# Queries and keys of an attention layer by fifteen products over thirds, in two passes of three heads, in place of seven products over halves in three passes of two

## The chip, the cores and the metric

One core of one Trainium2 chip. The metric is the device time of one run of the kernel, in microseconds, as the median of the runs shown. All numbers are float32.

## What is computed

Two graph layers over 128 graphs of 64 nodes with 768 features, 8192 rows in all. Each layer adds its attention's output to its input and normalizes.

```python
# layer 0: twelve heads of 64
h = jnp.einsum('bnd,ade->bane', feat_in, W); th = jnp.tanh(h)
attn = einsum(th, w_src) + swapaxes(einsum(th, w_dst), 2, 3)      # leaky, masked, softmax
feat_out = elu(einsum('banm,bame->bane', attn, h) + b)
gate = sigmoid(feat_in @ H_w.T + H_b)
x = layernorm(x + gate * feat_out + (1 - gate) * feat_in)
# layer 1: six heads of 128
q = heads(x @ Wq + bq); k = heads(x @ Wk + bk); v = heads(x @ Wv + bv)
probs = softmax(einsum('bhqd,bhkd->bhqk', q, k) / sqrt(128) + bias(mask), axis=-1)
x = layernorm(x + (einsum('bhqk,bhkd->bhqd', probs, v) merged) @ Wf + bf)
```

The change is in layer 1: how `x @ Wq` and `x @ Wk` are made, and what is ordered around them.

## The kernel before, in words

A tile is 128 rows (two graphs), a pair two tiles, a quad four tiles; there are 64 tiles, 32 pairs, 16 quads.

**Layer 0** runs over pairs: for each one the hidden product, the gate product and, two pairs behind, the product for layer 1's values, each over all 768 columns. Each is made by seven products of 384-wide halves instead of eight (the Strassen-Winograd form; `by_token`, L346, order in `TURNS`), each product three matmuls of 128x384. For the attention of each tile `attend` lists 33 steps on DVE, ACT, POOL, SP and PE. Transposes of rows and of weights go through DMA, on 2-byte halves of the numbers. When a pair is normalized, its transposed rows and their sums go to DRAM as the seven operands of the next layer (`ops_there`, L825 to L827), its values to `v_there`.

**Layer 1** runs over quads. Three times for each quad (`f` = 0, 1, 2), queries and then keys of two heads, `f` and `f + 3`, are made by seven products over halves (`by_feature`, L442: three matmuls of 128x256 each; `p1` to `p7` read the sums, two on ACT, five on DVE). After the last use of each of the seven blocks by `f` = 2, its `then` loads the block of the next quad into the same place in `zone` (L397). `slab` makes the scores of these two heads (L991), adds the mask (L1001), takes the softmax (L1005 to L1016), transposes the weights by DMA (L1031), makes the means (L1047) and transposes these by DMA (L1062) into the tiles `cT` (L1069). `output` makes the last product for two tiles at a time by fifteen products instead of eighteen: its contraction is cut in thirds, its columns in thirds, its rows in two (`FIFTEEN`; L1135, two matmuls of 128x256 a product, six sums in PSUM, of which two are taken up again by every third product). Every product is read and added to one or two of the six blocks of the result by DVE (L1148). Its operands on the side of the rows are sums that DVE makes (`operands`, L1102), those on the side of the weights sums that POOL makes once (L943). The rows that are added to come from DRAM (L1113), POOL adds the bias (L1118), and `normed` takes the statistics (DVE), the power (POOL, L370), the scaling (ACT, L1161) and the store.

**What sets the order.** Within an engine, instructions run in the order in which they were recorded. `Beat` sets it: a clock that runs on by one for every three matmuls; `beat.product` emits a product and sets its read 1.5 of its lengths later; lists of steps (`beat.start`, a `yield` is the pause) are emitted between the products at their times. It is an order alone, and the engines wait for each other through semaphores. All DMAs are issued by SP, one queue in that order. PSUM's eight banks: five for products, one for scores, two for means.

**At the border** of the layers the last pair's chain still runs while PE makes the values of the last pairs and, between these, queries and keys of quad 0; `matrix` loads and sums the weights of queries (POOL) and keys (DVE). **At the end** the two outputs of the last quad remain when the last scores are made; the operands of the first are DVE's, of the second mostly POOL's.

Of the kernel before, what the change touches and what calls it, by code (L numbers as in the profile page):

```python
# [54 lines left out]
P = 128  # L55
N = 64
# [18 lines left out]
PLACES = {X11: 0, X12: 1, X22: 2, S1: 3, S2: 4, S3: 5, S4: 6}  # L75

IN_ZONE = {X11: 0, S2: 1, S1: 2, X12: 3, S4: 4, X22: 5, S3: 6}


# [29 lines left out]


# [98 lines left out]
def two_layers(  # L209
# [68 lines left out]
    def matrix(w, name, engine, gap):  # L278

        t = places[place[name]]  # L280
        blocks = w.rearrange("(k c p) (m n) -> k m p c n", k=2, p=P, m=2)
        for at, k, m in ((W11, 0, 0), (T3, 0, 1), (W22, 1, 1), (W21, 1, 0)):
            for c in range(KH):
                nc.sync.dma_start(t[:, at, c], blocks[k, m][:, c])
                yield gap
        yield 3
        for to, a, b in ((T1, T3, W11), (T2, W22, T1), (T3, W22, T3), (N4, W21, T2)):
            for c in range(KH):
                engine.tensor_tensor(t[:, to, c], t[:, a, c], t[:, b, c], ALU.subtract)
                yield gap  # L290
        ready[f"{name}_sb"] = t


# [83 lines left out]
    ops_there = [dram.tile([P, 2, 7 * KH, P], F32, name=f"ops_there_{q}") for q in range(n_quads)]  # L377
# [3 lines left out]
    zone = const.tile([P, 7 * KH * 2 * P + 8 * P * 2], F32, name="zone")  # L381
# [10 lines left out]
    def load_block(q, k):  # L392

        at = PLACES[k] * KH
        t = in_zone(IN_ZONE[k] * D, KH, 2, P)
        for i in range(2):
            nc.sync.dma_start(t[:, :, i, :], ops_there[q][:, i, at : at + KH, :])  # L397
        return t.rearrange("p c i t -> p c (i t)")

    def queries(q, f, blocks, part):  # L400
        quads[q]["qT"] = in_zone(7 * KH * 2 * P, 2, 4 * P)
        by_feature(f"q_{q}_{f}_", blocks, ready["wq_sb"], f, bq_sb, quads[q]["qT"], part)

    def keys(q, f, blocks, part, then=None):
        quads[q]["kT"] = in_zone((7 * KH + 4) * 2 * P, 2, 4 * P)
        by_feature(f"k_{q}_{f}_", blocks, ready["wk_sb"], f, bk_sb, quads[q]["kT"], part, then)

    def by_feature(name, blocks, w, f, b_sb, r, part, then=None):

        sums = [sb(dense[0], [P, BANK], "dense", f"{name}{i}") for i in range(3)]  # L410
        begun = set()
        lo, hi = b_sb[:, f : f + 1], b_sb[:, f + 3 : f + 4]
        T = 2 * P
        u = {}

        def more(i, ps):
            u[i] = part(f"{name}u{i}")[:, 0:T]
            nc.vector.tensor_tensor(u[i], u[1], ps, ALU.add)

        def p1(ps):  # L420
            u[1] = part(f"{name}u1")[:, 0:T]
            nc.scalar.copy(u[1], ps)  # L422

        def p2(ps):
            nc.scalar.activation(r[:, 0, 0:T], ps, AF.Identity, bias=lo)

        def p7(ps):
            nc.vector.scalar_tensor_tensor(r[:, 1, T : 2 * T], ps, hi, u[3], ALU.add, ALU.add)

        def p4(ps):  # L430
            nc.vector.scalar_tensor_tensor(r[:, 0, T : 2 * T], ps, lo, u[1], ALU.add, ALU.add)

        def p3(ps):
            nc.vector.scalar_tensor_tensor(r[:, 1, 0:T], ps, hi, u[2], ALU.add, ALU.add)

        reads = dict(P1=p1, P2=p2, P3=p3, P4=p4, P5=lambda ps: more(3, ps), P6=lambda ps: more(2, ps), P7=p7)
        for what, to, xb, wb in TURNS:
            ps = sums[to][:, 0:T]

            def emit():  # L440
                for c in range(KH):
                    nc.tensor.matmul(  # L442
                        ps,
                        lhsT=w[:, wb, c, f * P : (f + 1) * P],
                        rhs=blocks[xb][:, c, :],
                        start=(c == 0 and to not in begun),
                        stop=(c == KH - 1),
                        skip_group_check=True,
                    )

            read = reads[what]
            beat.product(emit, lambda read=read, ps=ps: read(ps))
            begun.add(to)
            if then:
                then(xb)

    def phase_a(pa, ps_a, dst_pool):
# [25 lines left out]
        w_dst_sb = row(w_dst, "w_dst_sb", pa)  # L485
# [4 lines left out]
        w_src_sb = row(w_src, "w_src_sb", pa)  # L490
        h_b_sb = row(h_b, "h_b_sb", pa)
# [9 lines left out]
        for to, vector in ((bv_sb, bv), (bq_sb, bq), (bk_sb, bk)):  # L501
# [4 lines left out]
            [pa.tile([P, D], F32, name=f"{n}_{i}") for i in range(2)]  # L506
            for n in ("th_d", "bc_e", "xg_parts", "elu_turned", "gate", "mix")
        )
        h_of_tile = [pa.tile([P, H0, EP], F32, name=f"h_{i}") for i in range(3)]
# [300 lines left out]
        def sums_of_pair(p, begin):  # L810
# [12 lines left out]
            def away():  # L823
                there = ops_there[p // 2][:, p % 2]
                nc.sync.dma_start(there[:, 0 : 2 * KH], xo[:, 0:2].rearrange("p k c t -> p (k c) t"))  # L825
                nc.sync.dma_start(there[:, 2 * KH : 3 * KH], xo[:, 3])
                nc.sync.dma_start(there[:, 3 * KH : 7 * KH], so.rearrange("p k c t -> p (k c) t"))  # L827
# [79 lines left out]
    def phase_b(pb, ps_b):  # L907
# [75 lines left out]
        def slab(Q, f):  # L983
# [87 lines left out]
            if f == 2:  # L1071
                Q["done"] = True
# [181 lines left out]
```

## Time and profile before

| | us |
|---|---|
| three runs | 2860.69, 2854.07, 2859.43 |
| median | 2859.43 |
| the profiled execution: span from first to last instruction | 2857.3 |
| a pair of layer 0, steady | 42.75 |
| a quad of layer 1, steady | 87.8 |

The page gives no time for the profiled execution beside its span; it lies 2.1 us under the median and inside what the runs differ by. How to read it: PE is a matmul, PEld the load of its weights, which runs beside it. A float32 matmul has two records. L346 is any product of layer 0, L442 one of queries or keys, L1135 one of the output. A group's mean is the duration of one instruction from its start; on PE, where they overlap, its busy time divided by its records is nearer to what one costs. "Idle before" with a name behind it is the time in which the engine stood and what ended that. The waits are lines of who, for whom: total, times, longest.

### The profile page before, as it was taken

What the parts mean: (1) busy time and instruction counts of PE and PEld (TensorE: products, weight loads), DVE (VectorE), ACT (ScalarE), POOL (GpSimd) and SP (SyncE); (2) the same over time, 40 slices, a digit from 0 to 9 for tenths busy, and PEclk for the clock granted to TensorE, in tenths of its full rate; (3) what the DMA queues carried; (4) which work ended last, traced back from release to release, by engine and by line L of the source; (5) the groups of instructions that cost most, each with busy time, mean ns of one, the idle gap of its engine ahead of it and who ended that gap; (6) DMA issues with size and microseconds to landing.
All of it is one profiled execution on the core that took longest, in us unless ns stands there. A gap on an engine that the chain in (4) does not pass through costs nothing.

```text
span 2857.3 us, 43775 instructions
## 1 busy us (share of the span) xinstructions
PE 2803.1 (98%) x16168; PEld 2039.0 (71%) x16168; DVE 2042.6 (71%) x4103; ACT 1309.1 (46%) x1562; POOL 1063.8 (37%) x938
## 2 busy tenths in 40 slices
PE   7899999999999999999899999999999999999998
PEld 4555555555555555555588888888888888888886
DVE  6888888888888888888635556565555655556556
ACT  2655655655655655655423333333333333333331
POOL 5656656656656656666422101011011110110102
PEclk9999999999999999999999999999999999999999
DMA  6666666666666666667764345544355353554531
GB/s 202 160 167 175 171 173 171 177 163 173 179 162 175 178 167 170 178 167 191 206 156 117 97 110 128 128 95 107 100 132 135 92 122 85 123 135 99 124 87 58
DMA packets 627014, 409.59 MB, mean 143 GB/s; under 512 B 440177, under 2 KB 573041, under 8 KB 626801
## 3 DMA queue, kind: packets, MB, share of 16 engines
q1 hardware_dynamic: 626800, 406.81, 55.2%
q8 instruction: 127, 2.08, 0.3%
q14 instruction: 87, 0.70, 0.1%
HBM read 186.69 MB, written 119.93 MB: 107 GB/s over the span
## 4 chain that ended last, share of the span: by engine, by line
PE 90%; DMA 2%; DVE 2%; ACT 1%; issue 1%; SPq 1%; POOL 0%; POOLq 0%; DVEq 0%; ACTq 0%
PE o L1135 15%; PE q L442 14%; PE v L346 14%; PE h L346 14%; PE k L442 14%; PE g L346 14%; PE f_all L742 2%; PE s_ps L991 2%; PE c_ps L1047 2%; DMA s<-parts 1%; DMA th_d<-bc_e 0%; DMA elu_turned<-xg_parts 0%; DMA sT<-parts 0%; PE bias_ps L951 0%; DMA ops_there<-x_even 0%
## 5 line engine op out<-in xcount | busy, mean ns | idle before, releaser
L370 POOL TENSOR_TENSOR rs<-rs,power 128x1 f32<-128x1 f32 x128 | 73.8, 576 | 1097.3 <-DVE rs L368 1097.3
L346 PE MATMUL h<-w,zone 128*128 128x384 f32 x1320 | 447.9, 495 | 21.6 <-ACT h L533 12.5
L442 PE MATMUL q<-zone,w 128*128 128x256 f32 x2016 | 460.1, 383 | 4.7 <-issue 1.2
L346 PE MATMUL g<-w,zone 128*128 128x384 f32 x1320 | 441.0, 489 | 3.6 <-DVE gate L587 3.6
L442 PE MATMUL k<-zone,w 128*128 128x256 f32 x2016 | 443.2, 379 | 0.9 <-ACT k_u L422 0.9
L442 PEld LDWEIGHTS q<-zone,w 128*128 128x128 f32 x2016 | 379.8, 191 | 64.1 <-issue 8.7
L442 PEld LDWEIGHTS k<-zone,w 128*128 128x128 f32 x2016 | 383.2, 190 | 53.1 <-ACT k_u L422 1.3
L346 PEld LDWEIGHTS h<-w,zone 128*128 128x128 f32 x1320 | 251.3, 193 | 194.5 <-ACT h L533 13.8
L346 PEld LDWEIGHTS g<-w,zone 128*128 128x128 f32 x1320 | 247.9, 190 | 175.4 <-DVE gate L587 13.1
L1135 PE MATMUL o<-w,sc 128*128 128x256 f32 x1364 | 317.3, 381 | 5.0 <-DVE sc L1102 5.0
L1148 DVE TENSOR_TENSOR y<-y,o 128x256 f32<-128x256 f32 x512 | 207.2, 415 | 124.6 <-PE o L1135 119.8
L1135 PEld LDWEIGHTS o<-w,sc 128*128 128x128 f32 x1364 | 259.9, 191 | 41.6 <-DVE sc L1102 6.0
L346 PE MATMUL v<-w,x_sums 128*128 128x384 f32 x768 | 258.5, 487 | 1.7 <-DVE x_sums L315 1.6
L1118 POOL TENSOR_TENSOR y<-y,bf_sb 128x768 f32<-128x768 f32 x64 | 117.2, 1841 | 314.3 <-DMA y<-x_there 290.8
L662 POOL TENSOR_TENSOR bc_e<-th_d,w_dst_sb 128x768 f32<-128x768 f32 x64 | 120.7, 1886 | 292.3 <-ACT th_d L557 269.4
L346 PEld LDWEIGHTS v<-w,x_sums 128*128 128x128 f32 x768 | 145.8, 190 | 103.9 <-DVE x_sums L315 2.9
L1009 ACT ACTIVATE s<-s 128x512 f32<-128x512 f32 x48 | 30.2, 630 | 242.1 <-DVE s L1007 242.1
L1102 DVE SCALAR_TENSOR_TENSOR sc<-cT 128x256 f32<-128x256 f32 x217 | 116.6, 537 | 32.4 <-ACT cT L1069 32.4
L1061 ACT COPY parts<-c_ps 128x1024 uint16<-128x1024 uint16 x94 | 90.6, 1015 | 106.2 <-PE c_ps L1047 106.2
L657 POOL TENSOR_SCALAR zone<-zone 128x768 f32<-128x768 f32 x64 | 137.1, 2142 | 0.0
L1135 PE MATMUL o<-w,cT 128*128 128x256 f32 x512 | 132.6, 392 | 0.0
L650 ACT ACTIVATE gate<-gate 128x768 f32<-128x768 f32 x64 | 53.9, 843 | 167.6 <-DVE gate L593 118.6
(162 smaller groups left out, 4596.3 us busy)
## 6 DMA issues: line engine op xcount, KB each, us to landing
zone<-ops_there SPq DMA_DIRECT2D x224, 192.0 KB, 4.1
zone<-in_xT SPq DMA_DIRECT2D x32, 768.0 KB, 6.3
zone<-in_x SPq DMA_DIRECT2D x64, 384.0 KB, 3.8
bc_e<-there SPq DMA_DIRECT2D x128, 192.0 KB, 3.4
x_there<-mix SPq DMA_DIRECT2D x64, 384.0 KB, 3.9
ops_there<-x_sums SPq DMA_DIRECT2D x32, 768.0 KB, 3.3
v_there<-v SPq DMA_DIRECT2D x128, 192.0 KB, 2.6
v<-v_there SPq DMA_DIRECT2D x128, 192.0 KB, 3.8
```

Source lines behind the costliest of these rows:

```text
L346: nc.tensor.matmul(ps, lhsT=blocks[xb][:, c, :], rhs=w[:, wb, c, :], start=(c == 0 and to not in begun), stop=(c == KH - 1), skip_group_ch ...
L370: nc.gpsimd.tensor_tensor(rs[:, 0:1], rs[:, 0:1], power, ALU.pow)
L442: nc.tensor.matmul(ps, lhsT=w[:, wb, c, f * P : (f + 1) * P], rhs=blocks[xb][:, c, :], start=(c == 0 and to not in begun), stop=(c == KH - 1),
L657: nc.gpsimd.tensor_scalar(xs, xs, 1.0, None, ALU.add)
L662: nc.gpsimd.tensor_tensor(bc, th, w_dst_sb, ALU.mult)
L742: nc.tensor.matmul(f_all[b * N : (b + 1) * N, at : at + E0 + 1], lhsT=e[rows, hd // 2 * P + b * N : hd // 2 * P + (b + 1) * N], rhs=(h[row ...
L991: nc.tensor.matmul(s_ps[b * N : (b + 1) * N, i, r, :], lhsT=qT[:, r, at], rhs=kT[:, r, at], start=True, stop=True,)
L1061: nc.scalar.copy(by_halves(parts), halves(c_ps[:, r].rearrange("p i t -> p (i t)")))
L1102: nc.vector.scalar_tensor_tensor(s[:, k], of[a], sign, of[b], ALU.mult, op)
L1118: nc.gpsimd.tensor_tensor(y, y, bf_sb, ALU.add)
L1135: nc.tensor.matmul(ps, lhsT=of[xb][:, c, :], rhs=wf_sb[:, wb, c, :], start=(c == 0 and not begun), stop=(c == 1), skip_group_check=True,)
L1148: nc.vector.tensor_tensor(part_of, part_of, ps, ALU.add if sign > 0 else ALU.subtract)
```

## The change

Queries and keys are now made as the output is: fifteen products over thirds of the contraction, here with thirds for the three heads of a pass and two for the pairs of a quad. So there are two passes (`r` = 0, 1) of three heads. The first of a product's additions to a block is ACT's, with the bias, the others are DVE's. What goes to DRAM after layer 0 is the plain transposed rows; the eleven sums of them are POOL's, made for the whole quad from the loaded thirds in `zone` while the output of the quad before runs. For quad 0's first pass the eighteen plain products are made, from weights that are not yet summed. Two products have the sign of their weights turned, so that all of `X_SUMS` are plain sums. The scores of a pass stand after the second product of the next one, in two halves of three heads; the load of the next quad's mask stands beside them. The last tile rows, bias, pools' waits and the order at the border and at the end are changed with it.

```diff
+X_SUMS = (
+    ("3", "A0", "A2", ALU.subtract),
+    ("12", "3", "A3", ALU.add),
+    ("2", "A5", "A4", ALU.subtract),
...
+FREED = {"A2": "A2", "A5": "A5", "A3": "A3", "5": "A0", "A1": "A1", "6": "A4"}
...
+    def sums_of_quad(q):
+        there, made = quads[q].setdefault("raw", set()), set()
+        for name, a, b, op in X_SUMS:
+            while name in ("5", "6") and "raw_used" not in ready or not all(n in there or n in made for n in (a, b)):
+                yield 0.5
+            to, a, b = (operand(n).rearrange("p a b c -> p (a b c)") for n in (name, a, b))
+            nc.gpsimd.tensor_tensor(to, a, b, op)
+            made.add(name)
+            yield 0.5
...
+    def by_feature(name, w, r, b_sb, to_all, then=None):
+        sums, seen = {}, set()
+        for at, xb, wb, to in FIFTEEN:
...
+            def emit():
+                for c in range(2):
+                    nc.tensor.matmul(
+                        ps,
+                        lhsT=w[:, wb, c, r * P : (r + 1) * P],
+                        rhs=operand(xb)[:, c].rearrange("p i t -> p (i t)"),
+                        start=(c == 0 and not begun),
+                        stop=(c == 1),
+                        skip_group_check=True,
+                    )
...
+            def read(ps=ps, to=to):
+                for sign, b in to:
+                    m, n = divmod(b, 3)
+                    part_of = to_all[:, n, m * 2 * P : (m + 1) * 2 * P]
+                    if b in seen:
+                        nc.vector.tensor_tensor(part_of, part_of, ps, ALU.add if sign > 0 else ALU.subtract)
+                    else:
+                        seen.add(b)
+                        bias = b_sb[:, 3 * r + n : 3 * r + n + 1]
+                        nc.scalar.activation(part_of, ps, AF.Identity, bias=bias, scale=float(sign))
+            beat.product(emit, read, 2 / 3)
+            if then and xb in FREED:
+                then(FREED[xb])
...
             def away():
-                nc.sync.dma_start(there[:, 0 : 2 * KH], xo[:, 0:2].rearrange("p k c t -> p (k c) t"))
-                nc.sync.dma_start(there[:, 2 * KH : 3 * KH], xo[:, 3])
-                nc.sync.dma_start(there[:, 3 * KH : 7 * KH], so.rearrange("p k c t -> p (k c) t"))
+                nc.sync.dma_start(there, xo.rearrange("p k c t -> p (k c) t"))
...
-                beat.start(matrix(wq, "wq", nc.gpsimd, 0.6), 7)
-                beat.start(matrix(wk, "wk", nc.vector, 0.6), 14)
+                ready["wq_used"] = ready["wk_used"] = False
+                beat.start(first_blocks(), 4)
+                beat.start(by_head(wq, "wq", nc.gpsimd, 0.3), 7)
+                beat.start(by_head(wk, "wk", nc.vector, 0.5), 18)
+                beat.start(sums_of_quad(0), 21)
...
+        plain("q_0_0_", ready["wq_raw"], 0, bq_sb, qk[:, 0])
+        ready["wq_used"] = True
         value(n_pairs - 2)
-        queries(0, 0, blocks, part)
-        keys(0, 0, blocks, part)
+        beat.until(lambda: "wk_raw" in ready)
+        plain("k_0_0_", ready["wk_raw"], 0, bk_sb, qk[:, 1])
+        ready["wk_used"] = ready["raw_used"] = True
...
+        def slab(Q, r):
+            q, last = Q["q"], Q["q"] + 1 == n_quads and r == 1
+            if r == 1 and q + 1 < n_quads:
+                load(quads[q + 1])
...
+        for q in range(n_quads):
+            final = q + 1 == n_quads
+            if q:
+                queries(q, 0)
+                keys(q, 0)
...
+            beat.start(slab(Q, 0), 0.25)
+            if before:
+                beat.start(rows_of(before, 0))
+                beat.start(operands(before, 0))
+            queries(q, 1)
+            if not final:
+                if before:
+                    give(0)
+                beat.start(sums_of_quad(q + 1), 4)
+            if before:
+                beat.start(rows_of(before, 1))
+                beat.start(operands(before, 1), 6 if final else 0)
...
+            keys(q, 1, None if final else (lambda name: load_third(q + 1, name)))
+            beat.start(slab(Q, 1), 0.25)
+            if final:
+                beat.start(rows_of(Q, 0))
+                give(0)
+                beat.start(rows_of(Q, 1))
+                beat.start(operands(Q, 0), 1)
+                beat.start(operands(Q, 1), 6)
+            if before:
+                give(1)
             before, Q = Q, quads.get(q + 1)
+        give(0)
+        give(1)
...
-        tc.tile_pool(name="pb", bufs=1) as pb,
+        tc.tile_pool(name="pb", bufs=1, reuse_waits="tile") as pb,
```

`plain` is the same product without sums: for each half of the rows and each head six matmuls into one bank, read once by ACT. `give(i)` emits `output` for one half of the quad before, from its operands. So the passes of a steady quad are, in order: queries 0, keys 0, queries 1, first output, keys 1, second output. Each of the passes over queries or keys has fifteen products of two matmuls; the means of a pass stand in the passes after it, in two halves of three heads. Five banks of PSUM hold products, three scores, transposes and means.

## The prediction

> **What bounds the kernel now.** I read the page's busy table and its chain first, then the groups by form, then busy time by stretches, then the waits and the instructions of one quad in order of time.
>
> ```profile
> PE 2803.1 (98%) x16168; PEld 2039.0 (71%) x16168; DVE 2042.6 (71%) x4103; ACT 1309.1 (46%) x1562; POOL 1063.8 (37%) x938
> PE 90%; DMA 2%; DVE 2%; ACT 1%; issue 1%; SPq 1%; POOL 0%; POOLq 0%; DVEq 0%; ACTq 0%
> ```
>
> The chain that ended last is PE for 90%. The stretches (length, then busy PE, PEld, DVE, ACT, POOL with counts, clock, DMA share, GB/s) say where it isn't:
>
> ```profile
> 1351.41:1437.63 86.22, 74.81 (x343) 48.30 (x337) 57.07 (x102) 35.09 (x35) 35.01 (x32) 0.96 0.69 190
> 1621.64:1709.47 87.83, 87.83 (x566) 75.85 (x565) 51.48 (x123) 31.15 (x46) 10.59 (x12) 1.00 0.45 114
> 2796.82:2849.47 52.65, 47.13 (x249) 39.13 (x247) 36.37 (x89) 5.81 (x7) 13.46 (x19) 0.94 0.13 45
> 2849.47:2857.30 7.83, 0.00 (x1) 0.00 (x0) 2.44 (x10) 2.05 (x2) 1.49 (x4) 0.77 0.25 100
> ```
>
> The second row is one steady quad of layer 1: PE has no hole, DVE is busy for 59%, POOL for 12%. The first is the border of the layers, the third the end, the fourth the tail after the last matmul. So in layer 1 a matmul less is its time less, as long as no read of a product comes late.
>
> **What the skill says.** "SBUF — State Buffer", Who interferes with whom: a VectorE instruction with two SBUF inputs and a GpSimd instruction that reads SBUF exclude each other, whoever comes second waits for the whole instruction. The trace agrees: L1102 usually takes 0.42 us, and under a POOL addition
>
> ```profile
> 1640.51 1.81 POOL L1118 TENSOR_TENSOR y<-y,bf_sb 128x768 f32<-128x768 f32 x1 [5.15 <-DMA y<-x_there]
> 1640.78 1.82 DVE L1102 SCALAR_TENSOR_TENSOR sc<-cT 128x256 f32<-128x256 f32 x1
> ```
>
> "DMA: Bandwidth & Descriptors", Queues, rings and completion order: an issuing engine has one ring per DMA engine, consumed in order; so a small transfer stands behind large ones issued before it. The mask load had no such neighbours and still cost DVE 44.7/14 = 3.2 us a time (below). "TensorE: Matmul & The Clock Gate", Part 1: after some 3.4 us of idling the clock falls to half. The stretch 1400 to 1425, after a hole of 6.85 us, shows a granted clock of 0.87.
>
> **Part by part.** The rows I price with:
>
> ```profile
> L442 PE MATMUL k<-zone,w 128*128 128x256 f32 x2016 | 443.2, 379 | 0.9 <-ACT k_u L422 0.9
> L1148 DVE TENSOR_TENSOR y<-y,o 128x256 f32<-128x256 f32 x512 | 207.2, 415 | 124.6 <-PE o L1135 119.8
> L425 ACT ACTIVATE zone<-q,bq_sb 128x256 f32<-128x256 f32 x48 | 22.5, 468 | 66.5 <-PE q L442 66.1
> L943 POOL TENSOR_TENSOR w<-w 128x512 f32<-128x512 f32 x15 | 19.7, 1329 | 33.1 <-DMA w<-in_wf 32.7
> DVE biasb L972 <- DMA a8b<-in_adj: 44.7, 14, 5.1
> ```
>
> *Matmuls.* A matmul is two records; in the chain 42 records of k take 9.06 us, so 0.4314 us a matmul of 256 columns. A quad had 2 x 3 x 21 = 126 for queries and keys, and gets 2 x 2 x 30 = 120: 2.59 us less. Quad 0 gets 72 (plain) + 60 = 132. In all 2016 become 1932: 84 x 0.4314 = **-36.2 us**. Scores and means stay 96 matmuls a quad; groups of them stay six, so a quad without stalls is 87.8 - 2.6 = 85.2 us.
>
> *Reads.* A quad had 30 on DVE and 12 on ACT, and gets 40 of 0.415 and 24 of 0.469. DVE: 16.6 - 13.7 = +2.9 us of 85, ACT +6.3. Hidden as busy time. But a sum is now taken up again after two products (2 x 0.863 = 1.73 us), so a read that ends later holds PE. The output passes have lived on that distance already and PE waited for their reads only 0.5 us in all; there all reads are DVE's.
>
> *Sums by POOL.* 11 a quad of 1.33 us (L943) = 14.6 us in a row, during the second output pass, itself 14.6 us long (15 products of 0.863 and the scores, 1.08 x 1.5). They wait for the third loaded last; I count POOL ready about 17 us after the keys end, and the next queries need its late sums at 14.6 + 8.6 = 23 us. Not on the path in a steady quad. Its price is the exclusion above: two slab instructions of 128x768 (0.95 us, two SBUF inputs) can each be held up to 1.33 us, with reads queued behind.
>
> *The slab.* Two of 768 wide for three of 512: DVE 2 x 4.9 against 3 x 3.4 us, nothing. Its scores come after two products (1.73 us) where three of 1.29 covered the last keys before; one DVE read of 0.42 fits. The wait for the mask moves into the second output pass, ahead of that pass's first reads. I follow the pass: the load is issued about 0.9 us into it, behind 12 loads of 128 KB; it lands at 2.7 us if as quick as its 2.2 us so far, at 4.6 if it has to follow those (4.1 us; both medians from the page's DMA issues). The first read is needed at 4.2. Cost 0 to 1.1, and 0.3 for the exclusion: 0.3 to 1.4, I take 0.8.
>
> *ACT in the second keys pass.* Between the reads of products 8 and 10 stand one scaling (0.93) and two copies of 768 (L1069's pairs of 512 take 1.38, so 0.96 for one of 768). From 6.95 us: 0.38 + 0.93 + 1.92 + 0.47 + latency = 10.7, needed at 10.36: 0.36 us. In the first queries pass the transposed weights (issued at its start, 3.8 us to landing like the page's 12-block transpose th_d) come just ahead of need, 0 to 0.5, taken as 0.1. First keys, second queries and first output pass: 0. Sum **1.3 us a quad** (0.3 to 3), x 15 = **+19.5 us**.
>
> *SP, loads.* The 14 block loads become 12, spread over the second keys pass as slots come free; the writes of layer 0 shrink from seven blocks to four. Layer 0's order on PE is unchanged up to the last pair: 0.
>
> *Border.* Its 86.22 us held 9.87 + 3 x 13.54 + 2 x 9.06 + 2 x 1.06 = 70.7 us of products: 15.5 lost, most of it a weight transpose queued in SP behind ten zone loads (hole 6.85 us, and half clock after it). The loads are now early and the two plain passes are 15.5 us each, so these holes go. New ones: POOL makes 13 sums for wq (17.3 us) ahead of the power of the last tile, which I find ready at 71 us after the pair's begin and done at 82; scaling, transpose and copies end at 91.4, the last value product needs their sum at 89.5: 3.1 us. And in quad 1 no output pass covers POOL: its sums, with three of wf's between, end about 40.6 us after the second keys of quad 0 began, and the queries would be through at 37.8: 4.6 us. With 1.5 us of low clock 9.2: **-6.3**, from -12 to 0.
>
> *End.* 52.65 us held 90 output products' matmuls, a score group (1.28) and the last transposes and means (0.60 + 2.05): 90 x 0.4314 + 3.9 = 42.7: 9.9 lost to DVE making operands while PE waits. Now two output passes of the quad before (26 us) cover slab and operands (some 24.5 beats of 1.29 us, the first needed at beat 20), and POOL makes the second half. 2 us stay: **-7.9**. The tail of 7.83 us has the same steps.
>
> Sum: -36.2 + 19.5 - 6.3 - 7.9 = **-30.9**. The profiled execution spans 2857.3; the median of the runs, 2859.4, is 2.1 above that, which I leave: 2857.3 - 30.9 + 2.1 = **2828.5 us**.
>
> **Rivals.**
> 1. *All covered.* The mask lands in time and the reads hold, as they do in the output passes of before: no 19.5, so 2809. For: PE's waits for DVE there, 0.5 us. Against: ACT's 0.36 and POOL's lock follow from durations.
> 2. *Half eaten.* 2.7 us a quad (mask late, both locks met): +21, 2849.5.
> 3. *Slower.* The reads of the second output pass: DVE there has 16 x 0.335 + 5 us of slab + 3.2 of statistics = 13.6 us of 14.6, all behind the mask's wait, with POOL reading throughout. If the mask comes at 5 us or more and a lock is met at both 768 instructions, it can't catch up and PE follows it. It decides at (36.2 + 6.3 + 7.9) / 15 = 3.4 us a quad; at 4.5: 2859.4 + 67.5 - 50.4 = 2876.5. Against: in 1621 to 1709 two such locks of 1.4 us passed with PE at 100%.
> 4. *It doesn't do what it says*: out, since the order of the built kernel shows 966 matmuls each for q and k where there were 1008.
>
> **Chances.** Forecast (2818 to 2842) 0.42; rival 1 0.25; rival 2 (2842 to 2863) 0.18; rival 3 0.15. The range leaves out some of rivals 1 and 3: 2803 to 2865. A difference under 0.3% (8.6 us) can hardly be told from none here. Faster by more: 0.42 + 0.25 + half of rival 2 = 0.76; within: 0.10; slower: 0.14.
>
> **What would show it.** Right: a steady quad of 86.5 us (85.2 if rival 1, 88 or more if 2 or 3) with PE waiting for DVE reads of the second output pass and for ACT reads of keys; POOL at 30% in layer 1; the waits of the two-input slab instructions 1 us longer than bare; a hole of some 3 us before the last values and some 4 in quad 1's first queries; products until 8 us before the end. Wrong: a PE wait for transposed weights or for operands loaded late, a hole at the border of 10 us, or PE without holes in the steady quads at other than 0.43 us a matmul.

## The result and the profile after

The changed kernel takes 2844.27 us (median of 4 runs, 2841.36 to 2845.68) where the kernel before took 2858.61 (4 runs): a ratio of 0.9951, 95% interval 0.9937 to 0.9965. That is 14.3 us less; 30.9 were forecast. The profiled execution, the shortest of its four, spans 2839.6 us where before's spanned 2857.3: 17.7 less. The comparisons below are made between profiled executions and by stretch, since a median moves by 3 us from one set of runs to the next.

The page's busy table and chain, after:

```profile
PE 2777.5 (98%) x16002; PEld 2001.9 (71%) x16002; DVE 2111.3 (74%) x4182; ACT 1379.1 (49%) x1725; POOL 1316.8 (46%) x1119
PE 87%; DVE 5%; issue 2%; POOL 1%; DMA 1%; ACT 0%; SPq 0%; DVEq 0%; POOLq 0%; ACTq 0%
```

PE has lost 166 records and 25.6 us of busy time, and DVE stands in the chain with 5% where it had 2%: part of what PE no longer does is waited for instead. The same by stretches of the changed kernel: the border up to the last value product, one steady quad, the last 90 matmuls of the output (three passes of 15 products), the tail (length, then busy time of PE, PEld, DVE, ACT, POOL, the granted clock, DMA share, GB/s):

```profile
1351.41:1446.28 94.87, 85.35 (x396) 59.16 (x395) 61.29 (x92) 38.48 (x44) 59.96 (x46) 0.96 0.55 147
1696.49:1783.49 87.00, 86.14 (x553) 73.24 (x552) 54.66 (x129) 35.47 (x56) 26.65 (x24) 1.00 0.41 102
2783.73:2831.49 47.76, 46.02 (x232) 39.08 (x230) 33.58 (x93) 6.91 (x8) 16.72 (x25) 1.00 0.18 67
2831.49:2839.58 8.09, 0.00 (x0) 0.00 (x0) 2.44 (x10) 2.05 (x2) 1.48 (x4) 0.71 0.25 97
```

The steady quad takes 86.94 us on average (from one group of scores to the same group a quad later, over 13 quads), where 86.5 was forecast. By the same measure the kernel before takes 88.16, not the 87.8 of the single quad that the prediction started from, so the quad is 1.22 us shorter where 1.3 was forecast. In six of the runs below that leave the steady quads alone this figure is 87.0 to 87.2, so differences of 0.2 us a quad come from one execution to the next. POOL is busy for 30% in the quad. The border is not: PE lacks 9.5 of its 94.87 us. The rows that the prediction took its prices from held, but for POOL's sums, which took 1.43 instead of 1.33 us:

```profile
L520 PE MATMUL k<-zone,w 128*128 128x256 f32 x1860 | 414.3, 382 | 2.8 <-DVE qk L534 2.8
L538 ACT ACTIVATE qk<-k,bk_sb 128x256 f32<-128x256 f32 x186 | 88.3, 475 | 106.7 <-PE k L520 106.6
L474 POOL TENSOR_TENSOR zone<-zone 128x512 f32<-128x512 f32 x176 | 246.9, 1428 | 142.5 <-DMA zone<-ops_there 131.7
```

The wait of DVE for the mask (us in all, times, longest) was 44.7 us in 14 before, and is halved, though it now lies in an output pass:

```profile
DVE biasb L1052 <- DMA a8b<-in_adj: 21.2, 14, 4.9
```

**Where the 17.7 us come from.** Each term is the change of the time of that stretch, without what its larger or smaller number of matmuls accounts for:

| Term | Predicted | Measured | How measured |
|---|---|---|---|
| 84 fewer matmuls | -36.2 | -36.3 | records of each form x their undisturbed distance from start to start |
| layer 0 up to its last hidden product | 0 | -0.8 | its end, 1346.75 and 1345.99; over the other runs it lies at 1345.9 to 1348.2 |
| border, up to the last value product | -10.9 | -2.8 | 90.14 and 100.29 us, with 42 and 72 matmuls of quad 0 |
| steady stalls, and quad 1 | +19.5 + 4.6 | +24.9 | not measured by itself: the rest of the 17.7 |
| end, last 90 matmuls of the output | -7.9 | -3.0 | 52.65 us with scores and transposes in it, and 47.43 with 2.2 of these just ahead of it |
| tail | 0 | +0.3 | 7.8 and 8.1 us |

So 8 us are missing at the border and 5 at the end; the quads, where most of the argued risk lay, came out near the forecast.

**The border.** The largest hole in PE's timeline of the changed kernel, with the idle time ahead of the row and its releaser in brackets:

```profile
1401.64 0.34 PE L835 MATMUL f_all<-h,bc_e 64*64 64x65 f32 x1 [6.29 <-POOL w L341]
```

The hole before f_all, 6.85 us before, is there again with 6.29. The row names POOL's sums as its end; ACT's and SP's timelines, of which these are four rows, tell another story:

```profile
1385.93 1.47 ACT L819 COPY bc_e<-th_d 128x1536 uint16<-128x1536 uint16 x1
1391.70 3.83 SPq L328 DMA_DIRECT2D w<-in_wk  x6
1395.64 1.54 SPq L823 DMA_TRANSPOSE th_d<-bc_e  x1
1399.62 1.92 ACT L826 COPY bc_e<-th_d 128x1536 uint16<-128x1536 uint16 x1 [10.66 <-DMA th_d<-bc_e]
```

The block that is to be turned is ready at 1387.4. SP issues the loads of the key weights (each 0.6 us and more) and reaches the transpose at 1395.64; ACT's copy of what it brings ends at 1401.54, 0.1 us before f_all. The zone loads have left this place in SP's queue; the key weights' loads, begun at beat 18, have taken it.

**A steady quad.** PE's stalls in one quad of the changed kernel:

```profile
1704.54 5.45 PE L520 MATMUL q<-zone,w 128*128 128x256 f32 x24 [0.19 <-DVE qk L534]
1732.05 6.31 PE L520 MATMUL k<-zone,w 128*128 128x256 f32 x28 [0.18 <-DVE qk L534]
1748.37 1.99 PE L1230 MATMUL o<-w,sc 128*128 128x256 f32 x8 [0.48 <-DVE y L1243]
```

The brackets understate it. From start to start two records of PE (a matmul has two) are 0.216 us apart; at the first of these rows 0.57, and the next after it 0.32, so the stop costs 0.46. I sum this excess by pass; some 0.1 of each figure is the switch between kinds of matmuls, which the kernel before had too:

| us a quad | second queries | second keys | second output | scores to scores, us |
|---|---|---|---|---|
| changed kernel | 0.58 | 0.56 | 0.88 | 86.94 |
| y rows a pass earlier | 0.57 | 0.40 | 0.92 | 86.83 |
| maximum first | 0.14 | 0.29 | 0.90 | 86.38 |
| mask early | 0.57 | 0.56 | 0.70 | 86.79 |
| POOL's sums in halves | 0.57 | 0.57 | 0.30 | 86.37 |
| no sums by POOL | 0.57 | 0.57 | 0.11 | 86.17 |
| joined (below) | 0.10 | 0.28 | 0.23 | 85.68 |

The other three passes of a quad in the changed kernel, first queries, first keys and first output, have 0.13, 0.11 and 0.11, the switch alone. In runs that touch nothing in the second output pass its figure still varies, from 0.88 to 1.22.

### The profile page after: what moved, and what is told of

It reads as the page before. It is cut to its first block, busy times and chain, and to the rows that moved or that the text cites. A ratio compares the mean times of both kernels' runs of the same rounds, so it can differ in the third digit from the quotient of the medians.

```text
span 2839.6 us, 43938 instructions
## 1 busy us (share of the span) xinstructions
PE 2777.5 (98%) x16002; PEld 2001.9 (71%) x16002; DVE 2111.3 (74%) x4182; ACT 1379.1 (49%) x1725; POOL 1316.8 (46%) x1119
## 4 chain that ended last, share of the span: by engine, by line
PE 87%; DVE 5%; issue 2%; POOL 1%; DMA 1%; ACT 0%; SPq 0%; DVEq 0%; POOLq 0%; ACTq 0%
PE v L409 15%; PE h L409 14%; PE g L409 14%; PE k L520 13%; PE o L1230 13%; PE q L520 12%; PE f_all L835 2%; PE c_ps L1151 2%; PE s_ps L1080 2%; DVE s L1096 1%; DVE qk L534 1%; POOL zone L474 1%; DVE sc L378 1%; PE k L496 1%; DVE y L1243 1%
## 5 line engine op out<-in xcount | busy, mean ns | idle before, releaser
L520 PE MATMUL q<-zone,w 128*128 128x256 f32 x1860 | 420.8, 382 | 5.9 <-DVE qk L534 3.3
L520 PEld LDWEIGHTS q<-zone,w 128*128 128x128 f32 x1860 | 349.5, 190 | 63.4 <-DVE qk L534 10.2
L520 PEld LDWEIGHTS k<-zone,w 128*128 128x128 f32 x1860 | 350.2, 190 | 58.9 <-DVE qk L534 8.3
L474 POOL TENSOR_TENSOR zone<-zone 128x512 f32<-128x512 f32 x176 | 246.9, 1428 | 142.5 <-DMA zone<-ops_there 131.7
L534 DVE TENSOR_TENSOR qk<-qk,k 128x256 f32<-128x256 f32 x310 | 127.4, 419 | 207.5 <-PE k L520 203.4
L534 DVE TENSOR_TENSOR qk<-qk,q 128x256 f32<-128x256 f32 x310 | 125.7, 418 | 127.8 <-PE q L520 102.5
L755 POOL TENSOR_TENSOR bc_e<-qk 128x768 f32<-128x768 f32 x32 | 61.9, 1936 | 273.7 <-ACT qk L650 273.7
L1162 ACT COPY parts<-c_ps 128x768 uint16<-128x768 uint16 x124 | 97.1, 796 | 187.2 <-PE c_ps L1151 177.9
L538 ACT ACTIVATE qk<-q,bq_sb 128x256 f32<-128x256 f32 x186 | 86.2, 471 | 177.1 <-PE q L520 112.2
L538 ACT ACTIVATE qk<-k,bk_sb 128x256 f32<-128x256 f32 x186 | 88.3, 475 | 106.7 <-PE k L520 106.6
```

Source lines behind the costliest of these rows:

```text
L474: nc.gpsimd.tensor_tensor(to, a, b, op)
L520: nc.tensor.matmul(ps, lhsT=w[:, wb, c, r * P : (r + 1) * P], rhs=operand(xb)[:, c].rearrange("p i t -> p (i t)"), start=(c == 0 and not b ...
L534: nc.vector.tensor_tensor(part_of, part_of, ps, ALU.add if sign > 0 else ALU.subtract)
L538: nc.scalar.activation(part_of, ps, AF.Identity, bias=bias, scale=float(sign))
L755: nc.gpsimd.tensor_tensor(bc, th, w_dst_sb, ALU.mult)
L1162: nc.scalar.copy(of[:, i], halves(c_ps[i].rearrange("p n t -> p (n t)")))
```

## The experiments

The theory at the start: the quads lose what was forecast, by DVE reads that come late behind POOL's exclusion and the mask; the border loses to SP's queue; the end loses to slow means. Rivals stand with each run. Ratios are to the kernel before, with their 95% interval. Most of these intervals overlap that of the changed kernel, so what decides is the stretch that the edit touches. How far a stretch varies by itself can be read from the runs that do not touch it: the border (from the end of the last hidden product to that of the last value product) takes 99.2 to 101.7 us in the changed kernel and seven such runs.

**1. Key weights loaded later (wk_late).**

```diff
-                beat.start(by_head(wk, "wk", nc.vector, 0.5), 18)
+                beat.start(by_head(wk, "wk", nc.vector, 0.5), 27)
...
-                        yield gap
+                        yield 0.25 if name == "wk" else gap
```

> The changed kernel with one edit at the border: the 18 loads of the key weights begin 9 beats later and follow each other closely, so that they are issued behind the last weight transpose of layer 0 instead of ahead of it. Theory (the last sources' weight transpose stood about 8 us in SP's queue behind these loads): the hole of 6.29 us before f_all at 1401 falls to under 1.5 us, the granted clock after it stays near full, and the span falls from 2839.6 by 5 to 7 us. Rival (the hole belongs to POOL's sums for the query weights, which the trace names): hole and time unchanged. Second rival (loads just as late for the plain keys): the hole goes, and a wait of 3 to 6 us appears at L496 keys, so that the time stays.

Measured: 2843.69 us, 0.9952 (0.9939 to 0.9964), span 2840.8. The hole at f_all is gone, but the time is not gained: the border takes 99.42 us instead of 100.29, inside what it varies by. PE in this run, right behind the place of the old hole:

```profile
1408.90 4.21 PE L409 MATMUL v<-w,x_even 128*128 128x384 f32 x6 [3.80 <-DVE v L717]
```

SP's queue did make the hole; something else stood right behind it. It is not the second rival's wait: the plain keys (L496) run from 1412.90 to 1429.28 without one. DVE's read L717 waits in DVE's order behind three mixing steps of the last tile that take 1.36, 1.91 and 1.83 us, while POOL makes its sums for the query weights; the medians of these three steps (L860, L865, L378) over all 64 tiles are 0.95, 0.96 and 0.95.

**2. POOL's query sums behind the last power as well (border2)**: the edit of run 1 and, after the wait for `wq_used`:

```diff
+        if name == "wq":
+            yield 8
```

> The late loads of the key weights (as in the run before), and besides POOL's 15 sums for the query weights put behind the power of layer 0's last tile instead of ahead of it. Theory (two causes in series at the border: the weight transpose queued in SP, and then POOL's row of sums, which holds the last tile's power by 10 us and, by excluding DVE, its mixing, so that a fix of the first alone brings 1 us): the power of the last tile is done at about 1412 instead of 1421, the wait of 3.8 us for L717 falls under 1 us, and layer 0's last value product ends at 1439 to 1441 instead of 1446.3; span lower by 5 to 7 us. Rival (DVE's own work at the border is the bound, the reads and sums for the key weights): the last value product still ends at 1444 to 1446.

Measured: 2837.90 us, 0.9936 (0.9923 to 0.9948); the border 95.25 us, 5.0 less than in the changed kernel and nearly 4 under the shortest of the runs that leave it alone (the last value product ends at 1442.8, in an execution whose last hidden product ended 1.6 us later). POOL and DVE in this run:

```profile
1407.83 0.55 POOL L435 TENSOR_TENSOR rs<-rs,power 128x1 f32<-128x1 f32 x1 [7.43 <-DVE rs L433]
1408.61 21.57 POOL L343 TENSOR_TENSOR w<-w 128x512 f32<-128x512 f32 x15
1402.44 0.95 DVE L862 SCALAR_TENSOR_TENSOR mix<-elu_turned,mix 128x768 f32<-128x768 f32 x1
```

The last power, which ended at 1421.4 in the changed kernel, is there at 1408.4, and the mixing steps are at 0.95 again. A hole of 2.28 us is left, which ends at 1439.5 before a value product, with a lower clock behind it (0.86 from 1438 to 1450): DVE's sums for the key weights now run under POOL's 15, five of them in 8.44 us.

**3. POOL's query sums moved alone (wq_late)**: the edit shown under run 2, without that of run 1.

> The changed kernel with POOL's 15 sums for the query weights behind the last tile's power alone, the loads of the key weights left where the change put them. Theory (two causes in series: the transpose queued in SP first, POOL's sums after it): the hole at f_all of 6.3 us stays, the last power follows at about 1417 instead of 1421, and the last value product ends 0 to 2 us earlier, against 5 us with both edits and 0.9 with the loads alone. Rival (POOL alone is the cause, as the trace names it at the hole): the hole shrinks under 2 us and the last value product ends 4 to 5 us earlier with this edit alone.

Measured: 2845.61 us, 0.9965 (0.9953 to 0.9977); the border 102.91 us, 2.6 more than in the changed kernel, 1.2 above the longest of the runs that leave it alone. The hole stays:

```profile
1402.02 0.34 PE L837 MATMUL f_all<-h,bc_e 64*64 64x65 f32 x1 [6.79 <-issue]
1415.67 0.56 POOL L435 TENSOR_TENSOR rs<-rs,power 128x1 f32<-128x1 f32 x1 [16.07 <-DVE rs L433]
```

POOL has been idle for 16 us when the last power comes, so POOL's sums were not what f_all waited for, though the changed kernel's row said so. The theory had this edit at 0 to 2 us better; it is no better, and rather worse: a wait of 2.27 us for DVE's L719 has come in ahead of the last value product's last part. This profiled execution is the longest of its six. Neither edit alone gains anything that can be told from the spread; together they gain 5.0: the transpose comes first, POOL's sums second.

**4. Row halves alternating at the end (end_rows).**

```diff
-                    for i in range(2):
-                        c_ps = sb(ps_b, [P, 3, P], "x", f"c_ps_{q}_{r}_{h}_{i}", 3)
-                        rows = slice(i * N, (i + 1) * N)
-                        for n in range(3):
-                            for b in range(2):
+                    c_ps = [sb(ps_b, [P, 3, P], "x", f"c_ps_{q}_{r}_{h}_{i}", 3) for i in range(2)]
+                    for n in range(3):
+                        for b in range(2):
+                            for i in range(2):
+                                rows = slice(i * N, (i + 1) * N)
...
```

> The changed kernel with one edit at the end: the 48 matmuls of the last quad's means (L1126) alternate between the two halves of the rows, where they take 12 of one half and then 12 of the other. Theory (two matmuls on different row halves overlap, as those of before did: 32 in 2.05 us, now 48 in 5.4 us): the 48 take 2.8 to 3.1 us and the span falls by 2.3 to 2.6 us. Rival (they are slow because each group stands between output products and pays for the switch): 5 us and no change of the span above 0.5 us.

Measured: 2840.70 us, 0.9941 (0.9928 to 0.9953), span 2840.6. A group of means in the changed kernel, and, with the next wait of PE, in this run (some line numbers are higher by one; x counts records, two a matmul):

```profile
2785.88 1.55 PE L1126 MATMUL c_ps<-sT,v 64*128 64x64 f32 x12
```

```profile
2787.00 1.55 PE L1126 MATMUL c_ps<-sT,v 64*128 64x64 f32 x24
2806.39 1.13 PE L1231 MATMUL o<-w,sc 128*128 128x256 f32 x4 [2.06 <-DVE zone L1244]
```

That is twice the matmuls in the same time: matmuls on different row halves overlap. That is what the Trainium skill says in "TensorE: Matmul & The Clock Gate", Part 3 (packing small matmuls by row position), and the trace agrees. But the stretch of the last 90 matmuls of the output takes 47.32 us where it took 47.43: the 2.6 us came back as a wait for DVE, 2.06 us instead of 1.13, with a slower clock behind it.

**5. The statistics of the last but one quad later, on top of run 4's edit (end2).**

```diff
-                            beat.start(normed(y[k], 4 * q + 2 * k + i), 0)
+                            beat.start(normed(y[k], 4 * q + 2 * k + i), 4 if (q, i) == (n_quads - 2, 1) else 0)
```

> The changed kernel with the two row halves alternating in the last means, and the statistics of the last but one quad's last two tiles issued some 4 beats later, behind the first reads of the pass after them. Theory (the end follows DVE: the statistics and an operand held by POOL stand ahead of the reads that PE waits for, which is why faster means alone brought only a longer wait of 2.06 us): that wait falls under 0.5 us, and from the last keys to the last output product it takes 60 to 61 us instead of 64.2. Rival (the wait moves on to the operands of the last pass, which DVE makes): 63 us or more, with a wait named sc.

Measured: 2839.66 us, 0.9943 (0.9930 to 0.9957), span 2838.7; from the last keys to the last output product 61.5 us instead of 64.2, the last 90 matmuls 44.72. The wait is 0.69 us. So the end followed DVE: in the changed kernel two tiles' statistics (2 x 1.5 us) and an operand held for 1.75 us under POOL's bias addition stood ahead of the read that PE needed. The edit shows the part of the statistics; the operand is held in this run too, for 1.68 us. The later statistics without the faster means were not run.

**6. The y rows a pass earlier (rows_early).**

```diff
+            if q > 1:
+                beat.start(rows_of(before, 0))
             if q:
                 queries(q, 0)
...
+            if before:
+                beat.start(rows_of(before, 1))
             if not final:
...
```

> The changed kernel with the y rows fetched, and their bias added by POOL, one pass earlier: for the first output pass during the first queries and keys, for the second during the first output pass, where DVE runs no instruction with two SBUF inputs. Theory (POOL's addition of the bias holds a two-input operand or slab instruction of DVE, 2.0 instead of 0.42 us, and the read behind it comes late): the stall of 0.46 us in each second queries pass and of 0.46 us in each second keys pass goes, 0.9 us a quad, 12 us in all, and PE is not stopped anywhere else. Rival (DVE's own order of operands, slab and reads is too dense; my prediction blamed ACT's scalings and copies in the keys pass): stalls of 0.3 to 0.5 us stay at the same places and the time changes by less than 3 us.

Measured: 2837.07 us, 0.9930 (0.9917 to 0.9942), span 2836.0. Half of it failed: from scores to scores a quad gains 0.11 us where 0.9 was expected, and the two passes account for only a part of the 3.6 us of the span. In the second keys pass the changed kernel shows what was argued, an operand held by POOL's bias addition with a read behind it:

```profile
1641.02 3.58 POOL L1213 TENSOR_TENSOR y<-y,bf_sb 128x768 f32<-128x768 f32 x2
1642.93 1.95 DVE L378 SCALAR_TENSOR_TENSOR sc<-sc 128x256 f32<-128x256 f32 x1
1644.80 0.41 DVE L534 TENSOR_TENSOR qk<-qk,k 128x256 f32<-128x256 f32 x1
```

With the addition gone from there the operand takes 0.42 us and the stall falls from 0.56 to 0.40; what is left of it waits for an ACT read of the keys (13 waits of PE's weight loads for L538), the wait that the prediction had put there. In the second queries pass nothing changed, and DVE's order in this run says why:

```profile
1698.24 0.42 DVE L534 TENSOR_TENSOR qk<-qk,q 128x256 f32<-128x256 f32 x1 [2.19 <-PE q L520]
1698.58 0.42 DVE L378 SCALAR_TENSOR_TENSOR sc<-sc 128x256 f32<-128x256 f32 x1
1698.91 0.95 DVE L1094 TENSOR_REDUCE m<-s 128x12 f32<-128x768 f32 x1
1699.77 0.41 DVE L534 TENSOR_TENSOR qk<-qk,q 128x256 f32<-128x256 f32 x1
1700.10 0.42 DVE L378 SCALAR_TENSOR_TENSOR sc<-cT 128x256 f32<-128x256 f32 x1
1700.44 0.95 DVE L1096 TENSOR_TENSOR s<-s,m 128x768 f32<-128x768 f32 x1
1701.31 0.41 DVE L534 TENSOR_TENSOR qk<-qk,q 128x256 f32<-128x256 f32 x1
```

DVE idles 2.19 us at a read, with the slab's maximum, whose input has been there for 2.2 us, queued behind it. Then it has no pause for 3.5 us, and the third read is late.

**7. The maximum ahead of that read (slab_early)**, after each addition of the mask:

```diff
-                yield 1
+                yield 0.4 if r == 0 else 1
```

> The changed kernel with the slab's maximum (L1094) issued on DVE ahead of the first read of the second queries pass instead of behind it; the same instructions. Theory (DVE idles 2.2 us at that read while the maximum, whose input is there, stands behind it, and the reads after it then come late): the stall of 0.46 us in the second queries pass goes, 6 us in all. Rival (DVE has more work there than time, so that another read is late): the stall stays within 0.15 us.

Measured: 2837.28 us, 0.9939 (0.9926 to 0.9951), span 2839.6. The stall of the second queries falls from 0.58 to 0.14, as the theory had it, and that of the second keys to 0.29, which it had not; scores to scores 86.38. The span doesn't show it: this profiled execution is the longest of its five, quad 1's first queries lost 6.8 us in it instead of 3.8, and at the end PE waited 2.67 us instead of 1.13. A hole of 2.67 or 2.68 us stands there in runs 8, 9 and 10 too, none of which touches the end; what sets it was not tried.

**8. The mask half a quad earlier (mask_early)**: the load moved to the slab of the first pass, DVE's instruction left in place.

```diff
-            if r == 1 and q + 1 < n_quads:
+            if r == 0 and q + 1 < n_quads:
                 load(quads[q + 1])
+            if r == 1 and q + 1 < n_quads:
+                bias_of(quads[q + 1])
...
```

> The changed kernel with the next quad's mask loaded half a quad earlier, and the instruction of DVE that reads it left where it is. Theory (the reads of the second output pass start late because DVE waits for the mask): the waits of DVE for the mask, 21 us in all, go, the stall of that pass falls from 0.8 us on average to 0.2, 8 us in all. Rival (POOL's sums of the next quad hold the two 768-wide slab instructions at 1.7 us instead of 0.95, and the stall stands behind these): the wait goes, the stall stays at 0.6 or more, the time changes by less than 3 us.

Measured: 2844.34 us, 0.9952 (0.9938 to 0.9966). DVE waited for the mask 21.2 us in all, and now only once, for quad 0 (4.6 us); the stall of the second output pass falls from 0.88 to 0.70. The rival holds for most of it.

**9. No sums by POOL for quads 2 to 15 (no_sums).**

```diff
-            nc.gpsimd.tensor_tensor(to, a, b, op)
+            if q < 2:
+                nc.gpsimd.tensor_tensor(to, a, b, op)
```

> The changed kernel without POOL's 11 operand sums of quads 2 to 15 (left out: those queries and keys take whatever lies in the place of the sums). Theory (POOL's sums exclude the two-input slab instructions of the second output pass: L1096 and L1105 take 1.7 us there instead of 0.95): both take 0.95, the stall of that pass falls from 0.88 to 0.1 to 0.3 us a quad, 8 to 10 us in all. Rival (the late mask causes it): the stall stays at 0.6 or more.

Measured: 2832.86 us, 0.9919 (0.9906 to 0.9933), span 2831.0. The slab in a second output pass of the changed kernel, and in this run (lines one higher):

```profile
1652.34 15.42 POOL L474 TENSOR_TENSOR zone<-zone 128x512 f32<-128x512 f32 x11 [7.75 <-DMA zone<-ops_there]
1654.39 0.71 DVE L1052 TENSOR_SCALAR biasb<-a8b 128x256 f32<-128x256 uint8 x1 [1.96 <-DMA a8b<-in_adj]
1659.20 1.66 DVE L1096 TENSOR_TENSOR s<-s,m 128x768 f32<-128x768 f32 x1
1663.62 1.77 DVE L1105 TENSOR_TENSOR s<-s,r 128x768 f32<-128x768 f32 x1
```

```profile
1652.14 0.29 DVE L1053 TENSOR_SCALAR biasb<-a8b 128x256 f32<-128x256 uint8 x1 [1.60 <-DMA a8b<-in_adj]
1657.31 0.95 DVE L1097 TENSOR_TENSOR s<-s,m 128x768 f32<-128x768 f32 x1
1661.30 0.95 DVE L1106 TENSOR_TENSOR s<-s,r 128x768 f32<-128x768 f32 x1
```

Without POOL beside them both take 0.95 us and the stall is 0.11, though DVE waits for the mask as long as in the changed kernel or longer (28.0 us in all). The exclusion that the Trainium skill describes ("SBUF — State Buffer", Who interferes with whom) is the cause, and the mask matters only on top of it.

**10. POOL's sums in halves (halves).**

```diff
-            nc.gpsimd.tensor_tensor(to, a, b, op)
+            for at in (slice(0, 2 * P), slice(2 * P, 4 * P)):
+                nc.gpsimd.tensor_tensor(to[:, at], a[:, at], b[:, at], op)
```

> The changed kernel with each of POOL's operand sums in two instructions of 128x256 instead of one of 128x512. Theory (DVE's slab instruction waits for the rest of one POOL instruction, so shorter ones hold it for less): L1096 and L1105 in the second output pass fall from 1.7 to 1.2 to 1.4 us, the stall of that pass from 0.88 to 0.3 to 0.6 us, 4 to 8 us in all; POOL's sums of a quad take 15 to 17 us instead of 15.4. Rival (DVE loses to POOL at the next instruction again): durations of 1.6 us or more, no gain.

Measured: 2838.01 us, 0.9934 (0.9922 to 0.9947), span 2836.6. In the second output passes of quads 1 to 14 L1096 and L1105 take 1.23 and 1.28 us on average (0.95 to 1.57) where they took 1.72 and 1.66; the stall falls to 0.30; POOL's 22 instructions take 16.8 us instead of 15.4. That fits a DVE that waits for the rest of one POOL instruction.

**11. The output weights' sums behind quad 1's (wf_late).**

```diff
+            while not quads[1].get("operands"):
+                yield 1
             for to, a, b, op in W_SUMS:
...
-                yield 2
+                yield 1
```

> The changed kernel with POOL's 15 sums for the output weights behind its 11 sums for quad 1 instead of three of them between these. Theory (quad 1's first queries wait for POOL, as predicted at 4.6 us and seen at 3.8): the four holes at 1494 to 1502, each with POOL's L474 as its end, shrink from 3.8 us in all to 0 to 0.8. Rival (they wait for thirds loaded late): they stay above 2.5 us.

Measured: 2841.05 us, 0.9946 (0.9933 to 0.9960), span 2838.2. Quad 1's first queries lose 0.9 us instead of 3.8: the holes were POOL's, as predicted (4.6).

**12 and 13. Joined, without and with the early mask (joined_wf, joined_mask)**: runs 2, 5, 6, 7, 10 and 11 in one kernel.

> All the edits that shortened their place, together: late key weights and POOL's query sums behind the last power, row halves and late statistics at the end, y rows a pass earlier, the slab's maximum ahead of the first read, POOL's sums in halves, the output weights' sums behind quad 1's. If the causes are separate, the span falls by the sum of their parts: 5 at the border, 3 in quad 1, 2.7 at the end, and 0.45 + 0.3 + 0.4 a quad over 14 quads, 26 us, to 2812 to 2818. If they stand in one another's shadow (a read that is late behind two of them, the end's wait coming back), 2820 to 2830.

> The run before with the mask loaded half a quad earlier as well. With the holds by POOL shortened, the mask is the last thing in the second output pass: a stall of 0.1 us a quad there, 2 to 5 us less than without. If the holds still end last: within 2 us of the run without.

Measured: 2819.99 us, 0.9872 (0.9858 to 0.9885), span 2819.0; with the mask early 2819.35, 0.9869 (0.9855 to 0.9882). Both are faster than both kernels; the early mask adds nothing that can be told. A steady stretch of the joined kernel:

```profile
1700.00:1785.00 85.00, 84.97 (x551) 72.88 (x550) 50.87 (x129) 35.72 (x56) 27.28 (x34) 1.00 0.42 103
```

The border takes 93.6 us, the last 90 matmuls of the output 44.7. The span is 20.6 us shorter than the changed kernel's, between the 26 of causes that are separate and what was expected of causes in one another's shadow (2820 to 2830). What is missing is early in layer 1: quad 1's queries lose 4.7 us again, with holes that end with POOL's sums, and quad 0's first output pass 6.2 (1.7 in the changed kernel), with 3.35 us of it before an operand sc made by DVE. What orders that pass was not tried.

## Why the prediction was wrong

The sum was wrong by its border, and after that by its end.

*Matmuls* (-36.2): right, -36.3.

*The steady stalls* (+1.3 a quad): close in sum, in part by luck, and mixed in their reasons. The three stalls are 0.47, 0.45 and 0.77 us over the switch, 1.7 a quad, 0.4 more than was said. The forecast of the change still held, because the quads before lost time as well: they average 88.16 us, 0.36 over the quad that was taken as steady. The second output pass was put at 0.8 and measured 0.77, but with the mask as the larger part; runs 8 to 10 show POOL's exclusion as the cause, which adds 0.7 to 0.8 us to each of two instructions. One reading under the mask's price was wrong: the mask load of the kernel before did follow large transfers in SP's queue, two stores of the result (L1163) issued 2.6 and 0.4 us ahead of it in each steady quad. The second keys were put at 0.36 for ACT and measured 0.45 for an operand held by POOL's bias addition, with ACT's wait in its shadow (run 6). The second queries were put at 0 and measured 0.47: I counted DVE's busy time and not its order, in which the maximum stood behind a read that waited (run 7).

*Quad 1* (+4.6): near, 3.8, and for the reason given (run 11).

*The border* (-15.5 + 3.1 + 1.5 = -10.9 before quad 1, measured -2.8): this is the step that failed, for 8.1 of the 13.2 us that are missing between profiled executions. "The loads are now early and the two plain passes are 15.5 us each, so these holes go": the zone loads are early, but 18 loads of the key weights were put into SP's queue at the same place, and the transpose stood behind them as before. The prediction looked at what left the queue, not at what came into it. Behind this hole stands a second, which the prediction had (POOL's sums ahead of the last power, which waits 9.6 us for them in run 1) and priced at 3.1 us: while the first hole stands its removal brings nothing, with that hole gone it brings 4.2 us (runs 1 to 3). Together the two account for 5.0 of the 8.1 us; a hole of 2.28 us that is left in run 2 is part of the rest.

*The end* (-7.9, measured -3.0): two terms mis-sized. I took the last means at 2.05 us as in the kernel before, where 32 records alternate between row halves; the change makes 48 records in groups of one half, which take 5.4 us (run 4). And the stalls, said to be 2 us, are 3.2, since DVE's statistics stand in the way (run 5). Faster means alone bring nothing, since the wait for DVE takes up what they gain.

The rivals: all covered (2809) would have needed the quads at 85.2; the slower one needed 3.4 us a quad, and half of that was measured. The measured time lies in the range of "half eaten" (2842 to 2863) for another reason than that one gives: the quads did not lose the 2.7 us that it names. The median moved 3.4 us less than the profiled execution, which lies within the spread of the runs and is no step of the sum.

## What to carry to other kernels

A hole goes only if everything that stands in the queue ahead of the late step goes: list what a change puts in, not only what it takes out, and look for the wait that stands right behind the one removed, since an edit that closes a hole or shortens its place and brings nothing (runs 1 and 4) may have found the first of two. An engine at 60% can still be late: read its order, because an instruction whose input is ready costs nothing only if it does not stand behind one that waits. And long instructions on POOL are paid for by DVE's instructions with two inputs in SBUF; two short ones were cheaper here to have beside these than one long (run 10).

## What the runs showed of the hardware

A stop of PE costs more than its idle time: the record after the first one starts 0.32 us later instead of 0.22, so 0.10 comes on top (the stop at 1704.54 above). Longer holes can cost clock: in the end stretch 2800 to 2812 the changed kernel, with a hole of 1.13 us, ran at full clock, and the run with the maximum first, with a hole of 2.67, did not; there seven records in a row start 0.43 us after the one before, instead of 0.22. The stretch in both, first the changed kernel's:

```profile
2800.00:2812.00 12.00, 10.87 (x50) 9.02 (x49) 11.12 (x33) 2.06 (x2) 8.39 (x12) 1.00 0.14 57
```

```profile
2800.00:2812.00 12.00, 9.33 (x36) 7.60 (x35) 8.95 (x21) 2.06 (x2) 8.48 (x12) 0.86 0.17 66
```

The Trainium skill ("TensorE: Matmul & The Clock Gate", Part 1) gives some 3.4 us of idling for this; here shorter holes were followed by a lower clock: 1.73 us in the kernel before (at 2815), 2.06 in run 4, 2.28 in run 2 and 2.67 in runs 7, 8 and 9, each with a mean of 0.86 over 12 us around it. It did not happen each time: a hole of 2.68 us in run 10 and one of 2.27 in run 3 left the clock at 1.00.
